# Seven block products for the keys and queries of six head pairs of layer 1, with the sums between them in a new order

## The chip, the cores and the metric

The kernel runs on one core of one Trainium2 chip. The metric is the device time of one launch in microseconds (us). The engines are PE (TensorE, matrix products), DVE (VectorE), ACT (ScalarE), POOL (GpSimd) and SP (SyncE, which here only starts transfers). Each works through its own queue in program order.

## The reference

Everything is float32. Layer 0 is an attention over x (2 images of 512 channels and 2048 positions), an output projection and a residual. Layer 1 takes the positions as tokens, normalises each over its channels, and attends through landmarks; a linear map of a second norm follows. What matters here is the start of layer 1:

```python
t = _to_tokens(x)                                  # 2 x 2048 x 512
qkv = _ln_t(t) @ Wqkv                              # 512 -> 3 * 512
q, k, v = heads of 64 channels, 8 heads;  q = q * 64 ** -0.5
qL = q.reshape(b, h, m, l, d).sum(axis=3) / l      # m = 256 landmarks of l = 8 tokens
kL = k.reshape(b, h, m, l, d).sum(axis=3) / l
attn1 = softmax(q @ kL.T);  attn2 = softmax(qL @ kL.T);  attn3 = softmax(qL @ k.T)
out = attn1 @ (pinv(attn2) @ (attn3 @ v)) + depthwise_conv(v)
t = t + out @ Wout + bout
```

The pseudo-inverse is six rounds of products, started with the largest row and column sum over all heads and both images, so all landmark scores must exist before any round begins.

## The kernel before, in words

A pair is two heads, 128 channels; there are 4 pairs for each of 2 batches. Tokens come in 4 blocks of 512 (`NTB`, `TB`), channels in 4 chunks of 128 (`KC`). The program order of PE, DVE, ACT and POOL is the order in which the code emits instructions; generators that `yield` between steps are advanced in turns to mix two strands of work. Only the order of transfers on SP is left to the scheduler.

The first half of the run is layer 0. When its last attention ends, batch 1 still needs layer 0's output projection (`out0_units`, 16 groups of 4 matmuls, added to x at line 975) and the norm of layer 1 (`norm0_steps`, lines 986 to 1027: partial sums, a mean product, a subtraction over 2048 elements, squares on ACT, a variance product, a square root on ACT, a reciprocal on DVE, and a multiply that DVE and POOL share). Beside this the kernel works on layer 1 of batch 0:

- `keys_and_queries` (1231) takes one pair. For each token block and for keys and then queries it makes four matmuls into one PSUM bank (1245), a copy to SBUF on ACT (1248), a store to DRAM through SP, the landmark sums over 8 tokens (1250) and the largest magnitude (1253) on DVE. After the last block the landmarks are scaled and stored (1258) and bounds are formed (1262 to 1270).
- `attend` (1274) makes the landmark scores of a pair (1286), their exponential on ACT (1293), and on DVE row sums, reciprocals, the scaling and the sums again (1297 to 1303). `gram` (1305) multiplies the result with itself (1313), and ACT copies it out (1320).
- `others` (1777) runs pairs 1 to 3 of a batch, with `front` (`attend` and two `gram`s) of the previous pair woven into the next pair's products by `beside` (1768). Pair 0 of batch 0 has been done under the last attention of layer 0; pair 0 of batch 1 comes between the two runs of `others`.
- In batch 1, `second_of_first` (1877) begins the second pass (values, attn3, convolution) of the first pair beside `others`.

A loop over the 4 token blocks fixes how `out0`, `norm0` and `others` take turns. In it PSUM is split into two shared banks ("pp"), two double banks for scores ("sc"), two single banks ("av0", "av1") and two for products ("pr"); after it into four shared banks, two single ones and two for products. Weights of layer 1 have three slots of 128x4x128 and keys and queries two slots of 128x2048.

Of the kernel before, what the change touches and what calls it, by code (L numbers as in the profile page):

```python
# [10 lines left out]
F32 = mybir.dt.float32  # L11
# [646 lines left out]
BAND = P + 2 * HALO  # L658

GAP = object()  # L660


@with_exitstack
def fast_path(
# [350 lines left out]

    def norm0_steps(b, t, xb, xn, part):

        toks = slice(t * TB, (t + 1) * TB)
        name = f"n0_{b}_{t}"
        squares = lambda: (xb[:, :2, :], xb[:, 2:, :])  # L1020
        for rstd in statistics(xb, xn, part, name, squares, lambda: deviation(name)):
            yield
        nc.vector.reciprocal(rstd, rstd)
        wide = rstd.unsqueeze(1).to_broadcast([P, 2, TB])
        nc.gpsimd.tensor_tensor(xn[:, 2:, :], xn[:, 2:, :], wide, ALU.mult)
        nc.vector.tensor_tensor(xn[:, :2, :], xn[:, :2, :], wide, ALU.mult)
        nc.gpsimd.dma_start(chunked(xh_d[b])[:, :, toks], xn)
        yield
# [175 lines left out]
    def write_bands():  # L1204
# [6 lines left out]
        for h in range(HEADS):  # L1211
            nc.sync.dma_start(band_d[h].rearrange("(p q) -> p q", q=BAND + 1), rows[:, h, :])

    class Pair:

# [4 lines left out]

        def load_w(self, j):
            w = wpool1.tile([P, KC, P], F32, tag="w", name=f"w{j}_{self.name}")
            lo = j * HEADS * D + self.hp * P
            nc.sync.dma_start(w, chunked(wqkv[:, lo : lo + P]))
            return w


        def begin(self):
            self.w = {j: self.load_w(j) for j in (1, 0)}

        def keys_and_queries(self, pool, tag, xhs, after=lambda t: None):

            big = small.tile([P, 2, NTB], F32, tag="big", name=f"big_{self.name}", bufs=3)
            most = small.tile([P, 4], F32, tag="most", name=f"most_{self.name}", bufs=3)
            self.L = [
                lmpool.tile([P, LM], F32, tag=f"L{j}", name=f"L{j}_{self.name}") for j in range(2)
            ]
            k = kvpool.tile([P, S], F32, tag="k", name=f"k_{self.name}")
            q = pool.tile([P, S], F32, tag=tag, name=f"q_{self.name}")
            for t in range(NTB):  # L1240
                toks, marks = slice(t * TB, (t + 1) * TB), slice(t * TB // POOL, (t + 1) * TB // POOL)
                for j, dst, dst_d in ((1, k, k_d), (0, q, q_d)):
                    pp = bank(f"pp{j}_{self.name}_{t}")
                    for c in range(KC):
                        nc.tensor.matmul(  # L1245
                            pp, lhsT=self.w[j][:, c, :], rhs=xhs[t][:, c, :], start=c == 0, stop=c == KC - 1
                        )
                    nc.scalar.copy(dst[:, toks], pp)  # L1248
                    nc.sync.dma_start(dst_d[self.b, self.hp][:, toks], dst[:, toks])
                    nc.vector.tensor_reduce(  # L1250
                        self.L[j][:, marks], dst[:, toks].rearrange("p (m l) -> p m l", l=POOL), AX.X, ALU.add
                    )
                    nc.vector.tensor_reduce(
                        big[:, j, t : t + 1], dst[:, toks], AX.X, ALU.max, apply_absolute_value=True
                    )
                    if t == NTB - 1:
                        L = self.L[j]
                        nc.vector.tensor_scalar(L, L, (1.0, D**-0.5)[j == 0] / POOL, None, ALU.mult)
                        nc.sync.dma_start(L_d[self.b, self.hp][:, j, :], L)
                    yield  # L1260
                after(t)
            nc.vector.tensor_reduce(most[:, :2], big, AX.X, ALU.max)
            for j in range(2):
# [10 lines left out]
        def attend(self):  # L1274

            i, L = self.i, self.L
            scs = [scores_bank(f"sc2_{i}_{h}")[:, 0, :] for h in range(2)] if i + 1 < NPAIR else None
            X = self.X = [zpool.tile([P, 2, LM + 1], F32, tag=f"M{h}", name=f"X_{i}_{h}") for h in range(2)]
            rs = small.tile([P, 4], F32, tag="rs2", name=f"rs2_{i}")
            for h in range(2):  # L1280
                nc.vector.memset(X[h][:, :, LM:], 1.0)
            for h in range(2):
                rows_h = slice(h * D, (h + 1) * D)
                sc = scs[h] if scs else bank(f"sc2_{i}_{h}")
                for t in range(2):
                    nc.tensor.matmul(
                        sc[:, t * LM : (t + 1) * LM],
                        lhsT=L[0][rows_h, t * P : (t + 1) * P],
                        rhs=L[1][rows_h, :],
                        start=True,  # L1290
                        stop=True,
                    )
                nc.scalar.activation(X[h][:, :, :LM], sc.rearrange("p (t n) -> p t n", n=LM), AF.Exp)
            for h in range(2):
                two = slice(2 * h, 2 * h + 2)
                x_h = X[h][:, :, :LM]
                nc.vector.tensor_reduce(rs[:, two], x_h, AX.X, ALU.add)
                nc.vector.reciprocal(rs[:, two], rs[:, two])
                nc.vector.tensor_tensor(
                    x_h, x_h, rs[:, two].unsqueeze(2).to_broadcast([P, 2, LM]), ALU.mult  # L1300
                )
                nc.sync.dma_start(X_d[self.b, self.hp, h], x_h)
                nc.vector.tensor_reduce(rsum[:, i, two], x_h, AX.X, ALU.add)

# [18 lines left out]

        def front(self):

            self.attend()
            yield 2
            for h in range(2):
                self.gram(h)
                yield 0  # L1330


        def prefetch_w(self):
            self.w2 = self.load_w(2)

# [431 lines left out]

    def beside(main, other):

        for n in main:  # L1770
            yield
            for _ in range(n):
                if next(other, other) is other:
                    break
                yield

    def others(b, xhs, last, after=lambda t: None):

        for hp in range(1, NPAIR):
            pair = pairs[b][hp]  # L1780
            pair.begin()
            units = pair.keys_and_queries(kvpool, "k", xhs, after if hp + 1 == NPAIR else lambda t: None)
            next(units)
            yield
            yield from beside(last.front(), units)
            yield from units
            last = pair


    next_xhs, over = [], False  # L1790

    def load_next(t):
        assert over
        next_xhs.extend(load_x(xh_d, 1, "xh", t, 1))

    more = [others(0, xhs, pairs[0][0], load_next)]
    b = B - 1

# [9 lines left out]
    def norm0(t):  # L1808
        part = apool.tile([P, 2, TB], F32, tag="acc", name=f"part_f0_{t}")
        return norm0_steps(b, t, xbs_[t % 2], xns_[t % 2], part)  # L1810

# [4 lines left out]

    drain(out0(0))
    last, norm = None, norm0(0)
    next(norm)
    for t in range(NTB):  # L1820
        more_out = [out0(t + 1)] if t + 1 < NTB else []
        advance(more)

        next(norm)
        advance(more_out or more)
        if last is not None:
            next(last)
        advance(more_out or more)
        next(norm)
        advance(more, 2 if advance(more_out, 2) else 4)  # L1830

        next(norm)
        last = norm
        while more_out:
            advance(more_out)
        if t + 1 < NTB:
            norm = norm0(t + 1)
            next(norm)
    advance(more)
    next(last)  # L1840
    over = True
    while more:
        advance(more)

    mT = block_of(mpool, "m", "mT1")
    nc.sync.dma_start(mT, mT_d)
    b1_sb = const.tile([P, KC], F32, name="b1_f")
    nc.sync.dma_start(b1_sb, b1)
    wo_sb = load_wo(wo1, "wo_f1")
    banks.close()  # L1850
# [3 lines left out]
    xhs = next_xhs  # L1854
    pairs[1][0].begin()
    units = pairs[1][0].keys_and_queries(kvpool, "k", xhs)
    next(units)
    drain(beside(pairs[0][-1].front(), units))
    drain(units)
# [35 lines left out]
    first = second_of_first()  # L1895
    for i, _ in enumerate(others(1, xhs, todo[0])):
        if i == 8:
            todo[0].prefetch_w()
            todo[0].prefetch()
        if i >= 10:  # L1900
            next(first, None)
    drain(first)
    todo[1].prefetch_w()
# [7 lines left out]
    advance(vals)  # L1911
    for n in todo[NPAIR - 1].front():
        advance(vals, n // 2)
    n_bounds = 3 * B * NPAIR
# [273 lines left out]
```

## Time and profile before

| | us |
|---|---|
| median of 3 runs | 2731.47 (2731.37 to 2732.44) |
| profiled execution, first to last instruction | 2730.4 |
| PE busy in it | 2688.2 |
| DVE busy | 1628.1 |
| ACT busy | 903.7 |
| POOL busy | 161.8 |
| line 1245, PE busy | 227.8 in 512 records |
| the stretch from layer 0's last output to batch 1's last pair | 1388 to 1722 |

The profile is one execution. A busy share says how much of the span an engine had an instruction in it; for PE, whose matmuls overlap, it says only that the queue did not run empty. A group of instructions is given as line, engine, operation, what it writes and reads, shape and count, then its busy time, the mean of one in ns, and the idle time of the engine just before it with what ended that. A float32 matmul leaves two PE records. In the window views the columns are the stretch, its length, the busy time of PE, PE's weight loads, DVE, ACT and POOL with their counts, PE's granted clock, and the share and rate of DMA. In the timelines they are the start, the duration, the engine, the line and the operation. A wait is given as the waiting group, the releasing group, the total, the count and the longest.

### The profile page before, as it was taken

The numbers are of one execution on the slowest core, as the hardware profiler recorded it, in microseconds if no ns is written. First come the engines' busy times: TensorE is split into PE (matmuls) and PEld (weight loads), VectorE is DVE, ScalarE is ACT, GpSimd is POOL, SyncE is SP. The second block draws the span as 40 slices with busy tenths as digits, with TensorE's granted clock in tenths as the row PEclk, the third lists the DMA queues.
The fourth block names the chain that finished last, engine by engine and source line by source line (L and its number), as shares of the span: only waits on it lengthen the run. The fifth ranks groups of instructions, "written<-read, shape, count | busy, mean of one in ns | idle before, by whom it ended". The sixth has DMA issues, their size and how long they took to land.

```text
span 2730.4 us, 41173 instructions
## 1 busy us (share of the span) xinstructions
PE 2688.2 (98%) x16994; PEld 1361.7 (50%) x16994; DVE 1628.1 (60%) x2087; ACT 903.7 (33%) x1352; POOL 161.8 (6%) x109
## 2 busy tenths in 40 slices
PE   9999999999999999999999999999999999999999
PEld 5343443434443334344344455777677666655344
DVE  3768777664557765656667544445544645465565
ACT  1434343434334334444422223223323222231210
POOL 0101101000001100000002000000000000000000
PEclk9999999999999999999999999999999999999999
DMA  4100000212111200012024632312212112121211
GB/s 147 43 10 24 28 21 24 86 36 70 32 65 56 97 24 21 24 40 77 24 89 167 207 120 93 103 33 90 79 37 63 59 44 97 34 71 42 89 39 48
DMA packets 111476, 173.99 MB, mean 64 GB/s; under 512 B 16176, under 2 KB 67888, under 8 KB 106672
## 3 DMA queue, kind: packets, MB, share of 16 engines
q1 hardware_dynamic: 105136, 150.00, 17.0%
q0 software_dynamic: 5440, 20.97, 2.1%
q8 instruction: 135, 2.21, 0.3%
q14 instruction: 61, 0.50, 0.1%
q10 hardware_dynamic: 704, 0.31, 0.0%
HBM read 90.87 MB, written 63.57 MB: 57 GB/s over the span
## 4 chain that ended last, share of the span: by engine, by line
PE 90%; DVE 5%; DMA 1%; SPq 1%; ACT 1%; issue 1%; POOL 0%; DVEq 0%; ACTq 0%; POOLq 0%
PE sc_f L1072 15%; PE av_f L1102 15%; PE pp L1245 8%; PE pb L1538 5%; PE pa L1538 5%; PE vp_f L953 4%; PE vp L953 4%; PE pp_k_f L905 4%; PE yp_g L968 4%; PE yp_f L968 4%; PE fp_g L1694 3%; PE pp_q_f L905 3%; PE sc L1367 2%; PE sc L1595 2%; PE av L1611 2%; PE av L1388 2%
## 5 line engine op out<-in xcount | busy, mean ns | idle before, releaser
L1090 DVE TENSOR_TENSOR acc_f<-acc_f,p_f 128x1024 f32<-128x1024 f32 x448 | 581.0, 1297 | 209.5 <-ACT p_f L1080 181.0
L1080 ACT ACTIVATE p_f<-sc_f 128x1024 f32<-128x1024 f32 x512 | 496.4, 1021 | 564.2 <-PE sc_f L1072 561.5
L1072 PE MATMUL sc_f<-q_f,k_f 64*64 64x512 f32 x4096 | 491.2, 595 | 2.7 <-ACT p_f L1080 2.7
L1102 PE MATMUL av_f<-p_f,v_f 64*64 64x512 f32 x4096 | 484.3, 589 | 0.0
L1102 PEld LDWEIGHTS av_f<-p_f,v_f 64*64 64x64 f32 x4096 | 156.6, 133 | 283.0 <-issue 283.0
L1072 PEld LDWEIGHTS sc_f<-q_f,k_f 64*64 64x64 f32 x4096 | 145.8, 133 | 285.6 <-issue 261.9
L1245 PE MATMUL pp<-xh,w 128*128 128x512 f32 x512 | 227.8, 597 | 0.7 <-ACT q L1248 0.7
L1538 PE MATMUL pa<-M 128*128 128x192 f32 (+1 forms) x640 | 153.2, 385 | 6.3 <-ACT M L1529 6.3
L1245 PEld LDWEIGHTS pp<-xh,w 128*128 128x128 f32 x512 | 94.8, 190 | 119.6 <-issue 113.0
L1538 PE MATMUL pb<-R 128*128 128x192 f32 (+1 forms) x640 | 149.3, 380 | 0.5 <-DVE M L1551 0.5
L1538 PEld LDWEIGHTS pa<-M 128*128 128x128 f32 x640 | 109.3, 195 | 27.8 <-ACT M L1529 9.4
L953 PEld LDWEIGHTS vp_f<-wv_f,x 128*128 128x128 f32 x1024 | 115.7, 192 | 13.5 <-issue 11.8
L953 PE MATMUL vp<-w,xh 128*128 128x128 f32 x1024 | 120.9, 277 | 0.0
L953 PEld LDWEIGHTS vp<-w,xh 128*128 128x128 f32 x1024 | 117.0, 192 | 7.2 <-issue 4.6
L953 PE MATMUL vp_f<-wv_f,x 128*128 128x128 f32 x1024 | 118.8, 277 | 0.0
L1538 PEld LDWEIGHTS pb<-R 128*128 128x128 f32 x640 | 106.5, 190 | 23.6 <-DVE M L1551 0.8
L905 PE MATMUL pp_q_f<-x,wq_f 128*128 128x512 f32 x256 | 114.2, 598 | 1.7 <-DMA x<-in_x_dram 1.2
L905 PE MATMUL pp_k_f<-x,wk_f 128*128 128x512 f32 x256 | 114.3, 599 | 1.5 <-DVE k_f L908 1.1
L968 PE MATMUL yp_g<-o,wo_f 128*128 128x512 f32 x256 | 114.8, 597 | 0.0
L968 PE MATMUL yp_f<-q_f,wo_f 128*128 128x512 f32 x256 | 113.6, 598 | 0.9 <-DVE xr_f L975 0.9
L1120 POOL TENSOR_TENSOR q_f<-q_f,rinv_f 128x512 f32<-128x512 f32 x32 | 45.6, 1426 | 1040.1 <-DMA rinv_f<-acc_f 785.4
L1694 PE MATMUL fp_g<-xn_g,mT 128*128 128x512 f32 (+1 forms) x232 | 99.8, 580 | 0.0
(210 smaller groups left out, 2718.7 us busy)
## 6 DMA issues: line engine op xcount, KB each, us to landing
xh<-xh_fd SPq DMA_DIRECT2D x12, 1024.0 KB, 5.5
rinv_f<-acc_f SPq DMA_DIRECT2D x256, 32.0 KB, 1.9
xr_f<-in_x_dram SPq DMA_DIRECT2D x8, 1024.0 KB, 5.3
x_fd<-xr_f POOLq DMA_DIRECT2D x8, 1024.0 KB, 4.8
xh_fd<-xn_f POOLq DMA_DIRECT2D x8, 1024.0 KB, 4.8
k_fd<-k SPq DMA_DIRECT2D x32, 256.0 KB, 2.8
q_fd<-q SPq DMA_DIRECT2D x32, 256.0 KB, 2.8
k<-k_fd SPq DMA_DIRECT2D x8, 1024.0 KB, 6.4
```

The source lines that it names most:

```text
L905: nc.tensor.matmul(pp, lhsT=w_sb[kind][:, k, cols], rhs=xbs[t][:, k, :], start=k == 0, stop=k == KC - 1)
L953: nc.tensor.matmul(vp[:, j * P : (j + 1) * P], lhsT=xb[:, k, j * P : (j + 1) * P], rhs=w_of(k), start=k == 0, stop=k == KC - 1,)
L968: nc.tensor.matmul(yp, lhsT=wo_sb[:, k, m * P : (m + 1) * P], rhs=oTs[k][:, toks], start=k == 0, stop=k == NPAIR - 1,)
L1072: nc.tensor.matmul(sc[r * D : (r + 1) * D, h, :], lhsT=hd.k[rows, lo : lo + D], rhs=hd.q[rows, t * TB : (t + 1) * TB], start=True, stop=True,)
L1080: nc.scalar.activation(p, sc, AF.Exp, scale=D**-0.5)
L1090: nc.vector.tensor_tensor(acc, first if c == 1 else acc, p, ALU.add)
L1102: nc.tensor.matmul(av[r][half, :], lhsT=hd.v[keys, c, half], rhs=pp[keys, h, :], start=c == 0, stop=c == NST - 1,)
L1245: nc.tensor.matmul(pp, lhsT=self.w[j][:, c, :], rhs=xhs[t][:, c, :], start=c == 0, stop=c == KC - 1)
L1367: nc.tensor.matmul(scs[h][:, j * LM : (j + 1) * LM], lhsT=self.k[rows, c * P : (c + 1) * P], rhs=self.L[0][rows, :], start=True, stop=True,)
L1388: nc.tensor.matmul(self.av3[half, :LM], lhsT=self.v[:, c, half], rhs=self.p3[s][:, h, j * LM : (j + 1) * LM], start=c == 0, stop=c == NST - 1,
L1538: nc.tensor.matmul(dst, lhsT=lhsT[:, k, t * P : (t + 1) * P], rhs=rhs[:, k, :], start=k == 0, stop=k == 1)
L1694: nc.tensor.matmul(fp[:, cols], lhsT=mT[:, k, m * P : (m + 1) * P], rhs=self.xn[:, k, cols], start=k == 0, stop=k == KC - 1,)
```

## The change

Pairs 1 to 3 of both batches no longer compute keys and queries block by block. A unit (class `Unit`) is one pair and one half of the tokens, that is two blocks x0 and x1. Its result is a 2 by 2 arrangement, keys and queries against x0 and x1, and each entry was a sum of two half products, over the lower and the upper two channel chunks: 8 half products of two matmuls. They are replaced by Winograd's form of Strassen's seven products, with wk, wq the weights and lo, hi the channel halves:

| product | weights | tokens |
|---|---|---|
| 1 | wk_lo | x0_lo |
| 2 | wk_hi | x0_hi |
| 3 | s4 = wk_hi - s2 | x1_hi |
| 4 | wq_hi | t4 = x0_hi - t2 |
| 5 | s1 = wq_lo + wq_hi | t1 = x1_lo - x0_lo |
| 6 | s2 = s1 - wk_lo | t2 = x1_hi - t1 |
| 7 | s3 = wk_lo - wq_lo | t3 = x1_hi - x1_lo |

Bank u gathers 1, then 6, 7 and 4, and ACT copies it to SBUF after each of the four. DVE adds bank c (product 2) to the first copy, which gives the keys of x0; bank b (product 5) to the third, the queries of x1; then product 3 is gathered on top of 5 and b is added to the second copy, the keys of x1. The fourth copy is the queries of x0. Products 4 and 3 of a unit come after product 1 and 2 of the next. In batch 0, u is "av0" or "av1" in turn, c and b are halves of the two double banks "sc"; in batch 1, u is one of the two product banks, c and b are shared ones.

The token sums (class `Combined`) are four DVE operations of 128x1024 per half, made once per batch; the weight sums (`combine_w`) four of 128x256 per pair, of which one overwrites wq_lo. Stores, landmark sums and maxima of a unit now cover 1024 tokens. DVE work that nobody needs at once goes into the list `later`, maxima and bounds into `last_of_all`, and one entry is emitted after most products (`some`), or as many as a product needs (`until`). The string `ORDER` takes the place of the loop over token blocks: m is a step of layer 1, n one of the norm, o one of the output, a digit begins an output block. `attend` takes shared banks and returns its DVE steps as entries for `later`; `front` and `beside` are gone. The loads of the feed-forward map, the output weights and their bias move from between the batches into batch 1's run, some into other tiles.

```diff
+ORDER = "1mononmmnomomnnm2mnoonmnmnmoonmn3mmnoonmnmmnoommnnmnmmnmmnmmnmmmmnmmmmmn"
...
+    class Combined:
...
+            return [
+                call(5, t1, x1[:, lo, :], x0[:, lo, :]),
+                call(6, t2, x1[:, hi, :], t1),
+                call(7, t3, x1[:, hi, :], x1[:, lo, :]),
+                call(4, t4, x0[:, hi, :], t2),
+            ]
...
+        def combine_w(self):
...
+            return [
+                call(5, first, wq[:, lo, :], wq[:, hi, :], ALU.add),
+                call(6, lambda: self.few[:, hi, :], lambda: self.ws[5], wk[:, lo, :]),
+                call(7, wq[:, lo, :], wk[:, lo, :], wq[:, lo, :]),
+                call(3, lambda: room("s4")[:, lo, :], wk[:, hi, :], lambda: self.ws[6]),
+            ]
...
+    class Unit:
...
+        def product(self, to, m, start=True):
+            w, x = self.pair.ws[m], self.part.of[m]
+            for k in range(2):
+                nc.tensor.matmul(
+                    to, lhsT=w[:, k, :], rhs=x[:, k, :], start=start and k == 0, stop=k == 1, skip_group_check=True
+                )
+
+        def chained(self, m, row, t):
+            self.product(self.u, m, m == 1)
+            nc.scalar.copy(self.d[:, row, t, :], self.u)
+
+        def add(self, bank, row, t):
+            d = self.d[:, row, t, :]
+            nc.vector.tensor_tensor(d, bank, d, ALU.add)
+
+        def done(self, j):
...
+            *calls, most = self.pair.stored(j, self.tp, flat, toks)
...
+            later.extend(calls)
+            last_of_all.append(last)
+
+    later, last_of_all = [], []
+
+    def one():
+        (later or last_of_all).pop(0)()
...
+    def products(units, banks_of, between, meanwhile):
...
+        def fourth(u):
+            chained(u, 4, 1, 0)
+            u.done(0)
+
+        def third(u):
+            need(u, 3)
+            u.product(u.b, 3, False)
+            some()
+            u.add(u.b, 0, 1)
+            u.done(1)
+            if u.tp == 1:
+                last_of_all.append(u.pair.bounds)
+
+        last = None
+        for n, u in enumerate(units):
+            if n > 2 - u.pair.b:
+                until(lambda: not units[n - 3 + u.pair.b].left)
+            if u.tp == 0:
+                u.pair.begin_landmarks(2)
+            u.begin(banks_of)
+            chained(u, 1, 0, 0)
+            yield
+            if last:
+                fourth(last)
+                yield
+            u.product(u.c, 2)
+            some()
+            u.add(u.c, 0, 0)
+            between(u, 2)
+            yield
+            yield from meanwhile(u, 2)
+            if last:
+                third(last)
+                between(u, 3)
+                yield
+            chained(u, 6, 0, 1)
+            yield
+            need(u, 5)
+            u.product(u.b, 5)
+            some()
+            yield
+            chained(u, 7, 1, 1)
+            between(u, 7)
+            u.add(u.b, 1, 1)
+            yield
+            yield from meanwhile(u, 7)
+            last = u
...
+        def meanwhile(u, m):
+
+            hp = u.pair.hp
+            if m == 2 and u.tp == 1 and hp:
+                before = pairs[b][hp - 1]
+                until(lambda: all(before.marked))
+                later[:0] = before.attend()
+                yield
+            if m == 7 and u.tp == 1 and hp:
+                until(lambda: pairs[b][hp - 1].attended)
+                for h in range(2):
+                    pairs[b][hp - 1].gram(h)
+                    yield
...
+    norm = norm_of_all()
     next(norm)
...
+    for c in ORDER:
+        if c == "m":
+            advance(more)
+        elif c == "n":
             next(norm)
-    advance(more)
-    next(last)
+        elif c == "o":
+            if next(outs[0]) == KC - 1:
+                drain(outs.pop())
+        else:
+            outs.append((m for m, _ in enumerate(out0(int(c)))))
```

## The prediction

> **What bounds the kernel now.** I read the page first, then the windows by stage, the time-ordered chain of waits, PE's waits in the stretch the change touches, and the timelines of DVE and POOL there. First, sections 1 and 5 of the page:
>
> ```profile
> PE 2688.2 (98%) x16994; PEld 1361.7 (50%) x16994; DVE 1628.1 (60%) x2087; ACT 903.7 (33%) x1352; POOL 161.8 (6%) x109
> ...
> L1245 PE MATMUL pp<-xh,w 128*128 128x512 f32 x512 | 227.8, 597 | 0.7 <-ACT q L1248 0.7
> ```
>
> PE works through its in-order queue almost without a hole, so a product taken out of that queue shortens the run unless a wait replaces it. Line 1245 holds the keys and queries of all eight pairs. An f32 matmul is recorded as two PE instructions: 512 records are 256 products of 128x512, 32 per pair. Next the chain of waits, its piece for one run of this line:
>
> ```profile
> 1523.33 7.06 PE pp L1245 x16
> ```
>
> Eight matmuls in 7.06 us are 0.8825 us each (the mean of 597 ns per record overlaps its neighbour and is not a price). Then the windows, whose columns after the stretch are its length and each engine's busy time:
>
> ```profile
> 1388.00:1484.00 96.00, 95.60 (x238) 42.14 (x235) 63.19 (x74) 16.56 (x25) 12.55 (x9) 1.00 0.41 139
> 1484.00:1556.00 72.00, 68.20 (x192) 32.00 (x190) 45.77 (x84) 20.91 (x35) 8.72 (x7) 1.00 0.62 208
> 1556.00:1588.00 32.00, 32.00 (x91) 15.50 (x90) 16.69 (x37) 7.46 (x15) 0.00 (x0) 1.00 0.44 147
> 1588.00:1722.00 134.00, 134.00 (x650) 77.20 (x650) 58.37 (x115) 35.37 (x70) 0.00 (x0) 1.00 0.31 104
> ```
>
> The first two are batch 0's pairs beside layer 0's output and norms, the third is batch 1's first pair, the last batch 1's other pairs beside the first second-pass work. PE idles 0.4 + 3.8 = 4.2 us in all. DVE is 63.19 of 96 and 45.77 of 72 busy, which makes it the next limit. PE's waits from 1490 to 1640:
>
> ```profile
> PE pr L1313 <- DVE X L1299: 1.8, 1, 1.8
> PE pr L1313 <- ACT rstd_n L1008: 1.2, 1, 1.2
> PE pp L1245 <- ACT q L1248: 0.7, 1, 0.7
> ```
>
> These are the only waits there: 3.7 us. Last, two pieces of the DVE timeline and one of POOL's, which price DVE:
>
> ```profile
> 1438.37 1.22 DVE L1026 TENSOR_TENSOR xn_f<-xn_f,rstd_n 128x1024 f32<-128x1024 f32 x1
> 1439.51 0.74 DVE L975 SCALAR_TENSOR_TENSOR xr_f<-yp_f,b_f,xr_f 128x512 f32<-128x512 f32 x1
> 1440.17 2.71 DVE L1002 TENSOR_TENSOR xr_f<-xr_f 128x1024 f32<-128x1024 f32 x1
> ```
> ```profile
> 1438.47 3.33 POOL L1025 TENSOR_TENSOR xn_f<-xn_f,rstd_n 128x1024 f32<-128x1024 f32 x1 [16.37 <-DVE rstd_n L1023]
> ```
>
> From start to start an independent 128x1024 operation costs 1.14 us, and (from 1491.33, 1491.92 and 1492.52 of the same view) one of 128x512 costs 0.60. The third DVE line took 2.71 us where its like take 1.22: it ran while POOL's multiply ended at 1441.80.
>
> [...] reductions that nobody waits for precede the norm's work in program order at 1491. So an urgent add waits behind whatever is queued before it. [...]
>
> **The change part by part.**
>
> *PE, products.* Per pair 2 token halves x 7 products x 2 channel chunks = 28 matmuls replace 32. Over six pairs 24 go: 24 x 0.8825 = 21.2 us, all on the bounding queue. The built program has 168 such matmuls for 192; PE's order before the first and after the last of these pairs is the old one.
>
> *ACT.* Chained sums are copied out four times per unit (a pair and a token half), 8 per pair as before, 0.585 us each. Two more table loads, 2 x 1.28 us, because exponentials and the norm's square root alternate more often. ACT is 17 of 96 and 21 of 72 busy, so this lies beside PE; I take 0 (bounds 0 and 2.6 us if both stood in front of a copy that PE waits for).
>
> *DVE, added.* Token sums: 2 halves x 4 x 1.14 per batch, 18 us for both. Block adds out of PSUM: 3 per unit, 36 x 0.60 = 22 us. Weight sums: 24 of 128x256, [...] whose spacing I put at 0.35, 8 us. Removed: per pair 16 reductions of 512 (9.6 us) become 8 of 1024 (9.1), 3 us in all. Net +45 us. Only the order decides whether PE sees it, so I walked the built order in four stretches, with PE products of 1.765 us (two matmuls).
>
> *First half, up to the last output block of layer 0.* PE has about 88 us of work, DVE about 66. Adds come early. One wait: after the norm's reciprocal and multiply (from 50.4 us into the stretch: 3.3 + 1.2), the last token sum has two SBUF operands and is held until POOL ends, 2.2 us; the output adds behind it release the bank of the next variance product 1.6 us late. I take 2 us (bounds 0 and 5).
>
> *Second half, the rest of batch 0.* PE: 29 products x 1.765 = 51.2, 3 statistics at 0.88, two landmark score groups at 1.1 and two grams at 2.7: 61.4 us. DVE: 12 maxima and 10 landmark sums x 1.14 = 25.1; 13 block adds 7.8; 7 weight sums 2.5; two reciprocals 6.6, multiplies 2.3, a mean subtraction 2.2, partial and square sums 3.6; two landmark softmaxes 9 (4.5 each at 1525); bounds, scalings and copies 4: 63.1 us, and 2 x 2.2 held by POOL, 67.5. About 6 us may trail into the next stage, so the two engines are level, and what counts is what stands before an urgent add. The b banks of all units are one and the same buffer: the fifth product of a unit (into b) waits until the third product of the unit before is added out. In the second half of pair 2 that add stands behind four maxima (4.6 us), a landmark sum, a block add, the norm's square sums and the first softmax sum; PE arrives at 25.0 us of this stretch, the add ends at 30.1: a wait of 5.1. Before it, the landmark scaling is held by POOL: 2.3. A chunk copy that needs the recycled tile: 0.6. The weight sums behind the second reciprocal: 2. The same b bank one pair later: 1.5. Sum 11; as some of the trailing work may overlap, I take 10 (bounds 2 and 18).
>
> *Batch 1's first pair.* The weight sum of the next pair is queued behind bounds and reductions: PE arrives at about 36.4 us, the sum at 37: 1 us (bounds 0 and 3).
>
> *Batch 1's pairs.* DVE has about 83 us for PE's 132, and POOL is idle, so adds come in time. PE's four shared banks also hold c and b now, so grams and the attn3 scores wait for copies: 0.5 to 1 us at two or three places, 2 us (bounds 0 and 8). At the end four maxima and the bounds (6 us) now stand ahead of the last softmax: PE reaches the last gram 1.5 us early (bounds 0 and 4).
>
> *DMA.* Per pair the same bytes in half as many k/q stores; weights come when a slot is free, 256 KB in 3.3 us, with some 13 us until the sums need them. Loads of the projection map and output weights leave the hand-over for places under products. SP's queue has landmark stores, which wait for DVE, ahead of weight loads: if DVE runs 10 us late this cover is gone. I take 0.
>
> *Sum against the profiled execution.* No new wait can count below zero, since the old idle is given back in full here. The products give -21.2; the 4.2 us of old idle in this stretch belongs to an order that is replaced, so it goes; new waits 2 + 10 + 1 + 2 + 1.5 = +16.5. The net is -8.9: span 2730.4 - 8.9 = 2721.5. The median of the runs, 2731.47, is 1.1 over the span, so the prediction is 2722.6, which I state as 2722.
>
> **The rivals.** *Waits hidden (A).* If the bursts of maxima fall while PE still has slack, the new waits are 6 us: 2731.5 - 21.2 - 4.2 + 6 = 2712. For it: DVE's share is under its full time in three of four stretches. Against it: the second half has 67.5 us of DVE for 61.4 of PE.
>
> *The b bank takes it back (B).* The waits come to what they save: 25.4 us, 2731. For it: the upper bounds 5 + 18 + 3 + 8 + 4 = 38. This needs errors of one sign in several stretches.
>
> *DVE becomes the bound (C), slower.* One mechanism: each unit's fifth product waits for the previous unit's last add behind queued reductions. It decides from 25.4 / 11 reuses = 2.3 us per reuse. At the 5.1 us of the worst place in the five reuses of batch 0 and 2.5 in the other six, with the 2 us of the first half: 42.5, so 2731.5 - 25.4 + 42.5 = 2749. Against it: in batch 1 DVE has 63% of PE's time.
>
> *The products don't vanish (D).* The built program shows 24 fewer matmuls, so only a higher cost of each could undo it; they have the shape and operands of line 1245. I give it nothing.
>
> **How the numbers follow.** My case (2716 to 2726) 0.50, A (2708 to 2716) 0.25, B (2726 to 2737) 0.17, C 0.08. What this kernel's measurement can tell from no change is about 0.2%, 5.5 us: faster means under 2726.0, so 0.75; within, to 2737, 0.17; slower 0.08. The range 2710 to 2732 leaves out C, half of B's slower part and the low tail of A, together under 2 in 10.
>
> **What would show it.** Right: 168 matmuls in the new product line at 0.88 spacing; DVE near 90% from the last output block to batch 1; PE waiting for a DVE block add into b in pair 2, some 5 us, and for landmark scalings; batch 1 nearly whole. Wrong: PE full in the second half (then A), or waits over 2 us at every b reuse (C), or PE or DVE waiting for a weight's DMA.

## The result, and the profile after

The changed kernel took 2718.38 us (median of 5 runs, 2717.35 to 2719.35) where the kernel before took 2732.1 beside it: a ratio of 0.9949, 95% interval 0.9937 to 0.9961. That is 13.7 us less; the forecast was 9.5 us less. The profiled execution spans 2715.6 us for 2730.4. First the busy times of its page:

```profile
PE 2669.3 (98%) x16946; PEld 1353.2 (50%) x16946; DVE 1676.7 (62%) x2115; ACT 905.5 (33%) x1354; POOL 161.4 (6%) x109
```

PE is busy for 18.9 us less, DVE for 48.6 us more. Next the windows, as they were read before: beside layer 0's output, the rest of batch 0, batch 1's first pair, its other pairs, and the last gram.

```profile
1387.50:1475.50 88.00, 86.39 (x218) 38.95 (x215) 62.92 (x71) 17.89 (x26) 12.25 (x8) 1.00 0.32 114
1475.50:1545.20 69.70, 62.15 (x171) 28.80 (x169) 60.95 (x81) 20.90 (x35) 9.01 (x5) 1.00 0.70 242
1545.20:1577.40 32.20, 31.40 (x88) 15.30 (x89) 25.33 (x45) 6.47 (x13) 0.00 (x0) 1.00 0.51 173
1577.40:1706.60 129.20, 128.64 (x639) 73.99 (x637) 75.08 (x131) 36.20 (x71) 0.49 (x3) 1.00 0.33 113
1706.60:1722.70 16.10, 15.12 (x123) 14.24 (x123) 11.08 (x35) 4.13 (x9) 0.73 (x2) 1.00 0.73 254
```

PE's idle time is in the second row, 7.6 of 69.7 us, where DVE is busy for 61. PE's waits from 1380 to 1725 name it:

```profile
PE pu L1873 <- DVE s L1296: 2.8, 2, 2.2
PE sc L1368 <- DVE L L1336: 2.5, 1, 2.5
PE pb L1873 <- DVE kq L1883: 2.2, 1, 2.2
PE var_n L1008 <- DVE xr_f L977: 1.6, 1, 1.6
PE pr L1408 <- DVE X L1386: 1.0, 1, 1.0
PE pp L1275 <- issue: 0.9, 1, 0.9
PE pu L1873 <- ACT kq L1879: 0.3, 1, 0.3
```

Together 11.3 us: weight sums, landmark scaling, a block add, a variance product, the last softmax, and two small ones.

I measure the change by its own stretch, from layer 0's first output product (lines 968 before, 970 after) to the first pseudo-inverse product: 348.03 us before (1388.03 to 1736.06), 335.22 after (1387.52 to 1722.74), so 12.8 less. What follows in unchanged order went from 994.3 to 992.9 us. It has waits of its own that differ between executions, and I claim nothing from it. PE's granted clock is 1.00 in each of these windows of both kernels, so the clock has no part in this difference.

### The profile page after: what moved, and what is told of

The parts are those of the page before. It is cut to its first block, busy times and chain, and to the rows that moved or that the text cites. A ratio compares the mean times of both kernels' runs of the same rounds, so it can differ in the third digit from the quotient of the medians.

```text
span 2715.6 us, 41051 instructions
## 1 busy us (share of the span) xinstructions
PE 2669.3 (98%) x16946; PEld 1353.2 (50%) x16946; DVE 1676.7 (62%) x2115; ACT 905.5 (33%) x1354; POOL 161.4 (6%) x109
## 4 chain that ended last, share of the span: by engine, by line
PE 90%; DVE 6%; ACT 1%; DMA 1%; SPq 1%; issue 1%; POOL 0%; DVEq 0%; ACTq 0%; POOLq 0%
PE sc_f L1075 15%; PE av_f L1105 15%; PE pa L1624 5%; PE pb L1624 5%; PE vp_f L955 4%; PE vp L955 4%; PE pp_k_f L907 4%; PE fp_g L1780 4%; PE yp_g L970 4%; PE yp_f L970 3%; PE pp_q_f L907 3%; PE pu L1873 3%; PE sc L1453 2%; PE sc L1681 2%; PE av L1474 2%; PE pp L1275 2%
## 5 line engine op out<-in xcount | busy, mean ns | idle before, releaser
L955 PEld LDWEIGHTS vp_f<-wv_f,x 128*128 128x128 f32 x1024 | 115.7, 192 | 13.5 <-issue 11.8
L955 PE MATMUL vp<-w,xh 128*128 128x128 f32 x896 | 105.9, 277 | 0.0
L955 PEld LDWEIGHTS vp<-w,xh 128*128 128x128 f32 x896 | 102.1, 192 | 4.9 <-issue 3.0
L1686 ACT ACTIVATE p<-sc 128x512 f32<-128x512 f32 x128 | 66.6, 602 | 93.4 <-PE sc L1681 93.2
L1637 DVE SCALAR_TENSOR_TENSOR M<-M,pb 128x320 f32<-128x320 f32 (+1 forms) x160 | 60.1, 417 | 60.7 <-PE pb L1624 60.7
```

The lines of the kernel that those rows point to most:

```text
L955: nc.tensor.matmul(vp[:, j * P : (j + 1) * P], lhsT=xb[:, k, j * P : (j + 1) * P], rhs=w_of(k), start=k == 0, stop=k == KC - 1,)
L1637: nc.vector.scalar_tensor_tensor(out, m, scale, pr, ALU.mult, ALU.subtract)
L1686: nc.scalar.activation(p[:, h, :], sc, AF.Exp, scale=D**-0.5)
```

## The experiments

All start from the changed kernel. "Stretch" is the one just defined, from each profile. The theory at this point: 24 matmuls fewer are worth 20.6 us and the old idle of 4.2; 11.3 us go back in single waits, 10.1 of them for single DVE results that stand late in DVE's queue.

### Eight products in the new order

```diff
-            self.product(self.u, m, m == 1)
-            nc.scalar.copy(self.d[:, row, t, :], self.u)
+            to = {1: self.u, 4: self.c, 6: self.b, 7: self.u}[m]
+            w, x = self.pair.w[1 - row], (self.part.x0, self.part.x1)[t]
+            for k in range(KC):
+                nc.tensor.matmul(to, lhsT=w[:, k, :], rhs=x[:, k, :], start=k == 0, stop=k == KC - 1)
+            nc.scalar.copy(self.d[:, row, t, :], to)
...
```

Products 2, 3 and 5, their adds, the token sums and the weight sums go.

> The new order of the work stays (pairs spread between layer 0's output blocks and norms, landmark scores and grams at their new places, loads under products), but every one of the four results of a unit is made by four matmuls again: no token sums, no weight sums, no block adds, 192 matmuls instead of 168. Theory (the gain is products: 24 matmuls of 0.858 us fewer, 20.6 us, less 11.4 us of new waits of TensorE for sums, adds and scalings that stand late in VectorE's queue): the products come back, +20.6, and of the waits those for weight sums (2.8), the block add (2.2) and the variance product (1.6) must go and those for the landmark scaling (2.5) and the last gram (1.0) may stay: 2718.4 + 20.6 - 7 to 10 = 2729 to 2732, the time of the kernel before. Rival 1 (the new order is what gains, products net nothing because their adds cost as much as they save): 2722 or less. Rival 2 (the waits come from the order, not from sums and adds): they stay and it is 2736 or more.

Measured: 2736.92 us (2733.31 to 2740.12), a ratio to the kernel before of 1.0018 (1.001 to 1.0025); stretch 349.70. The order gains nothing by itself: its stretch is 1.7 us longer than before's, so rival 1 falls. The time is above my range and in rival 2's. Its reason holds for one part only, as PE's waits there show:

```profile
PE mean_n L992 <- DVE part_f L989: 2.9, 1, 2.9
PE var_n L1008 <- DVE xr_f L977: 1.8, 1, 1.8
PE av L1474 <- ACT p L1462: 0.7, 1, 0.7
PE pp L1275 <- ACT kq L1882: 0.7, 1, 0.7
```

They add up to 6.1 us, which the order makes without any sum or add, where the kernel before had 4.2. It is 5.2 less than in the changed kernel, and 20.6 - 5.2 = 15.4 against 14.5 measured (349.70 - 335.22). The variance wait is still there although no token sum exists, so it does not need one: here POOL's multiply holds one of the norm's square sums (2.23 us, 1.21 in the next norm). The rest of the 4.9 us over the kernel before lies outside the stretch, where the order is the same. Part of it is clock: from 20 to 40 us this execution was granted 0.91, the one before 1.00, by estimate 1.8 us (9% of the 20). Whether that belongs to this kernel, and what the remainder is, stays open.

### Seven products in batch 1 only

The same edit, under a test for batch 0; batch 1 keeps the seven products.

> Seven products in batch 1's pairs only; batch 0's pairs, beside layer 0's output and norms, by eight products in the new order, without token sums, weight sums and block adds there. Theory (products gain 10.3 us in each batch, the waits lie almost all in batch 0's share): against the changed kernel 10.3 us of products come back in batch 0 and 6 to 9 us of its waits go, so 2720 to 2723; batch 0's share of the change is worth only 1 to 4 us, batch 1's some 9. Rival (both batches gain alike, half of 13.7 us each): 2725. Rival (batch 0's share loses): under 2718.

Measured: 2723.68 us (2722.42 to 2727.28), stretch 340.96. That is 0.7 above my range, between theory and rival by time. The stretch shares it out: against eight products everywhere batch 1 gains 349.70 - 340.96 = 8.7 us of its 10.3, as the theory said, and batch 0 adds 340.96 - 335.22 = 5.7, where the theory had 1 to 4. Batch 0's waits cost a little under half of what its products save, less than I had put (6 to 9): the waits for the mean (2.9) and the variance (1.8) are in this kernel too.

### The c block's add first

```diff
             u.product(u.c, 2)
-            some()
             u.add(u.c, 0, 0)
+            some()
```

> Two lines exchanged: the add of the block in c is put into VectorE's queue right after its product, ahead of the queued sums and maxima that otherwise come between. Theory (the fifth product of pair 2's second unit waits for the c bank of its own unit, not for the b bank of the unit before, and the add stands only behind a landmark sum that waits for ScalarE and behind maxima): that wait falls from 2.24 to under 0.6 us and the time to about 2717 (2716 to 2718.5). The prediction's reason (the bank is that of the third product of the unit before, whose add this edit doesn't move ahead): the wait stays at 2 us or more, 2718.4. Rival (VectorE is the bound in this stretch, so the wait moves to the next product): the wait goes, the stretch is as long as before, 2718.4.

Measured: 2718.2 us (2717.32 to 2718.59), stretch 335.67. The wait for the block add is gone from the list, so the fifth product does wait for the c bank of its own unit. But nothing is gained: the variance product next in PE's queue now waits 1.44 us, for ACT, and the same exchange in earlier units makes new waits of 1.27 (a weight sum) and 0.47 us (a mean), of which a shorter variance wait returns 0.6. The rival's outcome, a wait that moves.

### No maxima

```diff
-                most()
+                nc.vector.memset(self.pair.big[:, j, self.tp : self.tp + 1], 0.0)
```

> Left out: the maxima over the keys and queries of the six pairs that are made from products (the input of their bound on magnitudes; a zero is written instead), 24 reductions of 128x1024, 27 us of VectorE. Theory (waits come from single places in an in-order queue): only the waits behind maxima go, for the block add (2.2) and for the last gram (1.0); those behind the norm's multiply on GpSimd stay (landmark scaling 2.5, weight sum 2.2, variance 1.6): 2718.4 - 3.2 = 2715 (2714 to 2717). Rival (VectorE is the bound of the second half, 61 of 70 us busy): all of the 9 us of waits there go, 2709 or less. Rival (another wait takes their place): 2718.

Measured: 2713.84 us (2712.83 to 2717.37), stretch 332.29. The waits that went are the block add, the last gram and a copy of 0.3; those that the theory kept are as long as before:

```profile
PE pu L1873 <- DVE s L1296: 2.8, 2, 2.2
PE sc L1368 <- DVE L L1336: 2.5, 1, 2.5
PE var_n L1008 <- DVE xr_f L977: 1.6, 1, 1.6
```

So 27 us of DVE work, 9.2 of them in the rest of batch 0, were worth 4.5, which is 0.2 beyond my range. The stretch shows only 2.9 less; in this execution the granted clock from 1520 to 1540, just behind the weight sum's wait, was 0.92, where the changed kernel has 1.00, by estimate 1.6 us (8% of the 20). DVE is not the bound of that stretch as a whole.

### The norm's multiply on DVE

```diff
-        nc.gpsimd.tensor_tensor(xn[:, 2:, :], xn[:, 2:, :], wide, ALU.mult)
+        other = nc.vector if apart else nc.gpsimd
+        other.tensor_tensor(xn[:, 2:, :], xn[:, 2:, :], wide, ALU.mult)
```

> The norm's multiply of its second half, 3.3 us on GpSimd, is done by VectorE instead for the four norms beside the pairs (1.14 us each, 4.6 in all), so that GpSimd holds nothing there. Theory (while GpSimd's multiply runs, the VectorE operation behind the norm's own multiply is held some 2.15 us[...]): the held operations fall back (landmark scaling 2.44 to 0.29 us, weight sum 2.56 to 0.42, token sum 3.37 to 1.22), each of the three waits behind them (1.6, 2.5, 2.2) is shorter by 2.15 - 1.14 = 1.0, so 2718.4 - 3 = 2715.4 (2714 to 2717). Rival 1 (another cause than GpSimd): the operations stay long, VectorE has 4.6 us more and it is 2720 or more. Rival 2 (VectorE is full there, so the added work takes back what the hold gave): 2718.

Measured: 2714.17 us (2713.22 to 2716.28), stretch 332.13, 3.1 less. DVE's timeline around the landmark scaling, first in the changed kernel, then here:

```profile
1490.10 1.22 DVE L1029 TENSOR_TENSOR xn_f<-xn_f,rstd_n 128x1024 f32<-128x1024 f32 x1
1491.24 2.44 DVE L1336 TENSOR_SCALAR L<-L 128x256 f32<-128x256 f32 x1
```

```profile
1489.68 1.23 DVE L1029 TENSOR_TENSOR xn_f<-xn_f,rstd_n 128x1024 f32<-128x1024 f32 x1
1490.82 1.22 DVE L1030 TENSOR_TENSOR xn_f<-xn_f,rstd_n 128x1024 f32<-128x1024 f32 x1
1491.96 0.29 DVE L1337 TENSOR_SCALAR L<-L 128x256 f32<-128x256 f32 x1
```

The scaling falls from 2.44 to 0.29 us. The waits behind it and its like:

```profile
1449.83 1.13 PE L1008 MATMUL var_n<-xr_f,mean_w 128*128 128x512 f32 x2 [0.59 <-DVE xr_f L977]
1494.36 1.14 PE L1369 MATMUL sc<-L,L 64*128 64x256 f32 x8 [1.46 <-DVE L L1337]
...
1517.68 1.96 PE L1874 MATMUL pu<-t_first,s 128*128 128x512 f32 x4 [1.23 <-DVE s L1297]
```

From 1.61, 2.53 and 2.24: each 1.0 shorter, as expected, and together all of the 3.1. POOL's multiply makes these three as long as they are: each time a hold of 2.15 us goes and 1.14 us of DVE's own work come in. An engine that is given more work makes the kernel faster here, because it had been held for longer than the work takes. This kernel beats both; its runs and the changed kernel's don't overlap.

### Two norm steps later

```diff
-ORDER = "1mononmmnomomnnm2mnoonmnmnmoonmn3mmnoonmnmmnoommnnmnmmnmmnmmnmmmmnmmmmmn"
+ORDER = "1mononmmnomomnnm2mnoonmnmnmoonmn3mmnoonmnmmnoommnnmnmmmmnnmmnmmmmnmmmmmmmn"
```

> Only the written order is changed: the last step of the third and of the fourth norm (reciprocal and multiplies) stands two places of the pairs' work later, so that pair 1's landmark scalings and pair 3's weight sum are ahead of the reciprocal in VectorE's queue, and a reduction with one operand follows the norm's multiply. Theory (these two waits, 2.5 and 2.2 us, are those operations queued behind 3.3 us of reciprocal and the hold): both go to under 0.4; the fifth product of pair 2's second unit is then reached 2.5 us earlier, while the c block's add still has the same VectorE work ahead of it less the hold of 2.15, so its wait of 2.2 stays or grows to 3.5: net -3 to -4.5, 2714 to 2715.5. Rival (VectorE sets the time of this stretch): 2717 to 2719, with the waits moved behind the reciprocal's new place. Rival (the later norm delays batch 1's input): the wait before batch 1's first product grows from 0.9 to 3 or more.

Measured: 2718.53 us (2717.07 to 2719.84), stretch 335.33: no gain. Both waits went to nothing, as the theory said, and came back elsewhere:

```profile
1501.99 3.26 PE L1873 MATMUL pb<-t_first,s 128*128 128x512 f32 x4 [4.09 <-DVE kq L1883]
1535.15 1.98 PE L1873 MATMUL pb<-t_first,s 128*128 128x512 f32 x4 [2.08 <-DVE X L1363]
```

The first is the block add, 4.09 for 2.24. The second is new, the same product one pair later (the profile names a small DVE operation that ended with the c block's add at 1535.09). That add ends 147.6 us into the stretch; in the changed kernel, where PE didn't wait for it, 147.0 (1534.53). PE only came to it earlier. The time is the rival's. The changed kernel's window from 1480 to 1500 shows one reason:

```profile
1480.00:1500.00 20.00, 17.07 (x44) 7.12 (x44) 19.56 (x18) 3.39 (x6) 4.17 (x2) 1.00 0.64 221
```

DVE is busy for 19.56 of 20 us. In such a piece an exchange pulls one result forward and pushes another back. There is a second reason in the first line: the product took 3.26 us where its like take 1.98. The window beside it has a granted clock of 0.91:

```profile
1500.00:1520.00 20.00, 17.95 (x47) 9.07 (x48) 14.09 (x26) 5.09 (x10) 2.08 (x2) 0.91 0.58 199
```

The waits of this kernel add up to 10.3 us for 11.3, so the exchange did return 1.0, and the slow product took it back. Behind that product DVE twice stood still for PE (2.83 and 0.64 us), so DVE was not the only limit here; how much the exchange is worth at full clock, no run shows.

### Both edits, for one unit

The later norms together with the c add first, the latter for batch 0's pair 2, second unit, alone.

> The two norm steps later, as in the kernel with only these moved, and for pair 2's second unit alone the c block's add ahead of the queued maximum and landmark sum. Theory: the waits for landmark scaling, weight sum and block add are all shorter; the variance product behind them waits for its adds, 1.4 us or a little more, as it did where all c adds were put first: 2712 to 2714.5. Rival (VectorE sets the time of this stretch): 2716 to 2718.

Measured: 2717.49 us (2716.41 to 2718.67), stretch 334.42. It ends with the rival: the block add's wait only falls from 4.09 to 2.97, and the new one of 2.08 stays. All waits add up to 9.2 us, 2.1 less than in the changed kernel, but the stretch is only 0.8 shorter, for here too the product behind the wait is slow:

```profile
1501.85 2.98 PE L1873 MATMUL pb<-t_first,s 128*128 128x512 f32 x4 [2.97 <-DVE kq L1883]
```

### Maxima made twice in pair 1 of batch 0

```diff
                 most()
+                if (self.pair.b, self.pair.hp) == (0, 1):
+                    most()
```

> The four maxima of batch 0's pair 1, which stand ahead of the c block's add of pair 2's second unit, are each made twice with the same result: 4 x 1.14 = 4.6 us more of VectorE at this place. Theory (from the landmark sum at 1485 to the block add at 1503 VectorE works without a hole and sets the time of this piece): the wait for the block add grows from 2.2 to 6.8 and the time to 2718.4 + 4.6 = 2723 (2722 to 2724). Rival (the added work falls into idle time further on, a wait behind it gets shorter): 2720 or less.

Measured: 2724.83 us (2722.78 to 2730.16), ratio to the kernel before 0.9975 (0.9966 to 0.9984), stretch 342.44. The mechanism holds, the sum doesn't. The fifth product starts 119.85 us into the stretch instead of 115.82, 4.0 later for 4.6 us of added work, in two waits:

```profile
1504.00 3.68 PE L1873 MATMUL pu<-t_first,s 128*128 128x512 f32 x4 [2.78 <-ACT kq L1879]
1509.75 2.67 PE L1873 MATMUL pb<-t_first,s 128*128 128x512 f32 x4 [2.07 <-DVE kq L1883]
```

The first is a copy on ACT into a tile that the maxima still read. The other 3.2 us of the stretch's 7.2 come later: slow products, as the 2.67 here for 1.98, the variance product behind it (1.91 for 1.10), and one of 3.60 for 1.96 after the next weight sum (the 3.68 above is made up for by a shorter wait). The runs spread over 7 us, and the clock goes with them: the four over 2728 us have a mean granted clock of 0.994 or 0.995, the other six 0.996 or 0.997. The profiled execution is one of the four; its clock from 1500 to 1520 is 0.83.

### Maxima made twice in batch 1

```diff
                 most()
+                if self.pair.b == 1 and self.pair.hp < NPAIR - 1:
+                    most()
```

> The eight maxima of batch 1's pairs 1 and 2 are each made twice: 8 x 1.14 = 9.2 us more of VectorE, twice as much as was put into batch 0, at places where VectorE is 58% busy. Theory (only what stands ahead of an urgent add in a full piece costs): no wait over 0.5 us more, 2718.4 (2717.5 to 2719.5). Rival (VectorE's work costs wherever bursts stand ahead of block adds): 2720.5 or more.

Measured: 2721.55 us (2721.3 to 2722.36), stretch 339.86. The theory is wrong here: 9.2 us of DVE work cost 3.2, though DVE is 58% busy. Of the 4.6 us that the stretch is longer, 1.7 lie in batch 0, which the edit doesn't touch: a product behind an unchanged weight sum's wait of 2.23 took 3.60 us for 1.96. The part that the edit does touch, from the first weight sum's wait in batch 1 (1581.60 in the changed kernel) to the last gram, is 2.9 us longer. DVE, ACT and PE there:

```profile
1662.10 4.85 DVE L1330 TENSOR_REDUCE big<-kq 128x1 f32<-128x1024 f32 x4
```
```profile
1667.11 1.07 ACT L1879 COPY kq<-pu 128x512 f32<-128x512 f32 x2 [8.44 <-PE pb L1873]
1668.07 1.10 ACT L1462 ACTIVATE p<-sc 128x512 f32<-128x512 f32 x2
```
```profile
1668.73 1.57 PE L1474 MATMUL av<-p,v 128*64 128x256 f32 x8 [1.84 <-ACT p L1462]
```

The maxima end at 1666.95. ACT's copy into a keys and queries tile starts then (the profile names a PE product, which writes another bank; in both kernels the copy starts 0.15 us after the maxima's end); an exponential stands behind the copy in ACT's queue, and PE waits for it. In the changed kernel the maxima there end at 1662.20, the copy starts at 1662.35, and PE's product at 1664.58 meets its exponential with almost no time left. So the larger part of the cost, 1.84 us, came not by a block add, as the rival had it, but through a recycled tile and ACT's order. The other 1.1 us are two groups of small products behind it that run longer (1.57 us for 1.08 and 1.70 for 1.14); no run shows why.

### The multiply on DVE, and one add first

The two edits named, the second for the one unit alone.

> The norm's multiply on VectorE, as in the kernel with only this, and for pair 2's second unit the c block's add ahead of the queued landmark sum. Theory (the landmark sum's 1.2 us and its 0.9 us of waiting for ScalarE leave the piece ahead of the add; the variance product behind is then held by ScalarE, 1.4 us, as where all c adds were put first): 2714.2 - 0.8 = 2713.4 (2712.5 to 2714.5). Rival (another wait takes all of it): 2714.2.

Measured: 2713.92 us (2713.33 to 2716.16), stretch 331.54, against 2714.17 and 332.13. By time this is no difference that 5 runs can tell, so theory and rival are not told apart; in the stretch, 0.6 shorter, the block add's wait of 2.24 is replaced by 1.44 before the variance product, as the theory expected.

## Why the prediction was right, and where it was not

The direction, the bound (PE's queue) and the size class were right, and the time is inside the range. Step by step:

- **Products, -21.2.** Right in kind. From start to start a product of two matmuls takes 1.72 us (1482.80, 1484.51 and 1486.23 in PE's timeline), 0.858 a matmul, so 20.6. The 7.06 us of the group counted the tail by which its last matmul overlaps the next instruction, the error the prediction avoided on DVE (1.14 for 1.22).
- **Old idle, -4.2.** Gone, as said. In the eight-product kernel the new order makes its own instead, so this gain and the waits below are one account.
- **First half, +2.** 1.61 measured, by the path that I named: POOL holds the token sum (3.37 us for 1.22), and the output adds behind it come late. The token sum itself is exchangeable, though. In the eight-product kernel, without token sums, a square sum is held instead (2.23 us for 1.21) and the wait is 1.8. What counts is the multiply on POOL: without it 0.59.
- **Second half, +10.** 7.3 measured (2.53, 0.27, 2.24, 2.24). The five terms that I summed to 11 add up to 11.5. Landmark scaling (2.3 forecast), the recycled tile (0.6) and the weight sum behind the reciprocal (2) were near. The failed step is "The b banks of all units are one and the same buffer: the fifth product of a unit (into b) waits until the third product of the unit before is added out." It was priced at 5.1 and 1.5 us. The two banks do not stay with c and b: this fifth product takes the one that its own unit's c leaves. DVE and PE of the changed kernel:

```profile
1495.98 4.59 DVE L1330 TENSOR_REDUCE big<-kq 128x1 f32<-128x1024 f32 x4
1501.46 1.22 DVE L1325 TENSOR_REDUCE L<-kq 128x128 f32<-128x1024 f32 x1 [0.89 <-ACT kq L1879]
1502.60 0.68 DVE L1883 TENSOR_TENSOR kq<-pc,kq 128x512 f32<-128x512 f32 x1
...
1505.87 0.67 DVE L1883 TENSOR_TENSOR kq<-pb,kq 128x512 f32<-128x512 f32 x1
```
```profile
1503.34 1.98 PE L1873 MATMUL pb<-t_first,s 128*128 128x512 f32 x4 [2.24 <-DVE kq L1883]
```

  The product starts when c's add ends at 1503.28. The add that I had named runs at 1505.87, after the product has begun, so it can't be what released it; and with c's add moved ahead, in the third experiment, the wait was gone. That a wait stands at this product at all is partly luck: c's add is behind the same four maxima that I had counted ahead of the other. With the true bank the wait is 2.24, and one pair later there is none, 2.24 for the 6.6 that I had priced.
- **Batch 1.** First pair 1, measured 1.4: 0.56 for the weight sum that I had named, and 0.86 before its first product, for which I had nothing and for which the profile names no cause. Other pairs 2, measured 0; the repeated maxima show that one place there has no time left. The end 1.5, measured 0.98.
- **Sum.** New waits 11.3 for 16.5. -20.6 - 4.2 + 11.3 = -13.5, against -12.8 in the stretch; 0.7 is not accounted for. The forecast gain of 8.9 falls 4.6 short of the 13.5: the waits were priced 5.2 too high, 4.4 of it at the b banks, and the products 0.6.
- **DVE +45, ACT and DMA 0.** 48.6 measured (the weight sums' spacing, my estimate of 0.35, is 0.33: 1520.50 to 1520.83 in DVE's timeline), and DVE is 87% busy in the rest of batch 0 (60.95 of 69.70), near the 90% that I had named; no wait for a table load (1.28 us each in both profiles) or a weight's DMA appears.
- **Rivals.** A, the waits hidden, put them at 6 us; they were nearly twice that. B needed 25.4 us of waits. C needed one at every reuse of b, and there was one in all.

My own theory after the result also lost a part: not single places alone, but one piece of some 30 us (1479 to 1508) in which DVE stands still for only 1.2. There taking work or holding out pays (multiply off POOL 3.1 us of stretch; no maxima 2.9, or by estimate 4.5 at full clock), and adding work costs. Reordering gave no time that the runs can tell in four attempts: in one other waits grew by as much as one shrank, in one 0.8 us of them went, and in two the 1.0 and 2.1 us that went were lost again, for the most part, to slow products.

## What to carry to other kernels

A product saved on the bounding engine is worth its start-to-start spacing (here 0.858 us a matmul), and what the sums for it take back is decided by a few results in one in-order queue, so read that queue where it is full and not its share over a stage. Where it has no hole, expect an exchange of its entries to move most of a wait and not to remove it: take work out, or find what holds it, and an operation that another engine does "for free" may be the one (here POOL's multiply: without it the stretch was 3.1 us shorter). Follow recycled banks and tiles to the actual last reader before a wait is priced; a wrong reader cost this forecast more than any duration did.

## What the runs showed of the hardware

- **The order.** DVE ran its queue as the code emits it: with c's add moved ahead of the queued sums and maxima the wait of 2.24 for it was gone, and with the reciprocal moved behind the landmark scaling the wait of 2.53 was. ACT did the same: in the kernel with batch 1's maxima made twice an exponential whose scores were done at 1663.26 started at 1668.07, behind the copy that had begun at 1667.11.
- **The hold.** POOL's multiply held the DVE operation right behind the norm's own multiply about 2.15 us, whether it reads two SBUF tensors (2.56 for 0.42, 3.37 for 1.22) or is a tensor_scalar with one (2.44 for 0.29); the last ended at 1493.68, POOL's multiply at 1493.53. A reduction in the same place ran in 1.21 in the eight-product kernel, its usual time, and the square sum behind it took 2.23 for 1.21.
- **The clock after a wait.** In four of the twelve profiles a product just behind a wait of 2.1 to 4.1 us was slow, up to 3.7 us for 1.98. One of them, in the kernel with pair 1's maxima made twice, kept PE for 3.44 us from its start to the next start, where the changed kernel has 1.79: about half the rate. The windows of 20 us in which these products began have granted clocks of 0.83 to 0.92, and the kernel without maxima has 0.92 behind its weight sum's wait, where the changed kernel has 1.00. The length of the wait alone doesn't decide: behind 2.53 before the landmark scores no product was slow in the changed kernel, and behind the same 2.53 one took 3.23 us for 1.98 in the kernel with batch 1's maxima made twice; behind a wait of 2.9 in the eight-product kernel the clock stayed at 1.00. What decides, no run shows. Such a wait cost up to 1.7 us more than it shows; the prediction had no term for that.
